# A graph layer on one core: 16 of the 128 columns of each copied group move to GpSimd

## The chip, the cores and the metric

The kernel runs on one core of a Trainium2 chip. The metric is the device time of one execution in microseconds (us). The engines are written as the profile writes them: PE (TensorE, the matmuls; PEld are its weight loads), DVE (VectorE), ACT (ScalarE), POOL (GpSimd) and SP (SyncE, which here only starts transfers). Each engine has a queue of its own, which takes the engine's instructions in their order; where it does something itself (loading addresses into registers, waiting for a second semaphore) the trace has rows for PEq, DVEq, ACTq and POOLq.

## The reference

One message-passing layer of a graph network with a residual and a layer norm, for 12,500 nodes of 64 features and 200,000 edges of 32 features. The edges come sorted by their target, `dst`.

```python
msg_in   = concatenate([x[src], x[dst], edge], axis=-1)      # 64 + 64 + 32 features
messages = relu(msg_in @ mW1 + mb1) @ mW2 + mb2              # 160 -> 128 -> 64
agg      = segment_sum(messages, dst, 12500)
upd      = relu(concatenate([x, agg], axis=-1) @ uW1 + ub1) @ uW2 + ub2
out      = layernorm(x + upd)                                # over the 64 features
```

## The kernel before

**Tables and tiles.** A first stage computes two tables in DRAM, `tab_a` = x times the source rows of mW1 and `tab_b` = x times its target rows with the bias, one row of 128 for each node. After that an edge needs only row `src` of `tab_a`, row `dst` of `tab_b` and its own 32 features times the edge rows of mW1. Edges are worked on in tiles of 128; six tiles are a group, and there are 261 groups. In the hidden layer a group is the PSUM tile `pc`, 128 edges by six blocks of 128.

**One group.** For each tile, `edge_part` issues one product over 64 rows (L413): 32 rows are edge features and the weights for them, 32 are a selection matrix and a window of `tab_b` (the edges are sorted, so one window of 32 nodes holds all targets of a tile). The rows of `tab_a` come by `fetch` (L241): an indirect transfer on POOL's queue for each tile, a *gather*, brings the 128 rows that `src` names into the tile `xg` in SBUF. `node_part` adds them to `pc` by a product with the identity matrix (L442), 384 wide for three blocks at a time. `positive` (L466, DVE) takes the relu into `h`; `collect` multiplies `h` by selection matrices and so sums the edges of each node in PSUM (L506), beside a product that counts them (L502). After some groups, `update` and the functions that follow it compute the second MLP and the layer norm for 416 nodes or so and store them.

**Copied groups.** In 121 of the 261 groups (`COPIED`) the last two of the six tiles aren't gathered. The kernel keeps x transposed in SBUF, twice: `xtop` holds the 64 features of each node on partitions 0 to 63 and zeros below, `xbot` the same on partitions 64 to 127 with zeros above. For each pair of edges, one of either tile, one column of `xtop` and one of `xbot` are added into one column of the tile `xc` (128 columns; three buffers). As the nodes are known only at run time, their addresses are loaded into registers from the table `col_a`, two for each column (`addresses`, L359). The tile `xc` is then multiplied by the source rows of mW1 (L416, two products of 64 rows for the two tiles, right behind L413 of the same tile). Such a group needs four gathers, not six, and its identity product is 256 wide.

**Who copies.** ACT copies the first `singles(j)` columns of copied group number j, 64 or (for one j in six) 72, by an activation with the second column as its bias (`singly`, L383). DVE copies the rest, by an or of the two columns (`joined`, L391). On both a load of 16 addresses stands in front of eight columns. POOL copies nothing.

**Pace.** The columns of a group are spread over several steps. `progress(s)` is the number of copied groups, with fractions, that are done after step s, by the rates in `PACE` (about half a group in each step); `portion(s, own)` gives the columns of an engine's share that fall on step s, rounded to eights (`CHUNK`). Copied group c is the one whose copying ends in step c - 3; the list is filled so:

```python
    while progress(s) >= len(COPIED) + 1 and s + 3 < FINAL:
        COPIED.append(s + 3)
```

**The main loop.** The order within each engine is the order in which the code is written (nothing is reordered). Step s of 258 issues, in turn: the gathers of group s + 8, the transfers of windows of `tab_b` for group s + 2, `node_part(s)`, `collect(s - 1)`, DVE's columns in three or four parts with the selection matrices and the relu of group s between them, `edge_part(s + 1)`, and ACT's columns. The gathers of a step are tied to products of that step: the first is free, the second waits for L442 of group s, the others for products of `collect(s - 1)` (and, where there are six, of `edge_part(s + 1)`). So POOL's gathers run about eight groups ahead of their use, in a pace set by TensorE. A tile `xg` may be refilled once its reader is done.

The functions that the change touches:

Of the kernel before, what the change touches and what calls it, by code (L numbers as in the profile page):

```python
# [10 lines left out]
F32 = mybir.dt.float32  # L11
I32 = mybir.dt.int32
AF = mybir.ActivationFunctionType
ALU = mybir.AluOpType
AX = mybir.AxisListType
ET = mybir.EngineType

P = 128
# [57 lines left out]
OFFS = 4  # L76
SBASE = (33556480, 33554432)
CBASE = 33566720
PACE = ((3, 0.474), (50, 0.501), (130, 0.479), (170, 0.465), (261, 0))
FINAL = 258  # L80
SUMMED = 255

# [1 line left out]
def progress(s):  # L84

    return sum(r * max(0, min(s + 1, b) - a) for (a, r), (b, _) in zip(PACE, PACE[1:]))

# [8 lines left out]

def singles(j):

    return 72 if j % 6 == 0 else 64

# [27 lines left out]
def gnn_kernel(ctx: ExitStack, tc: tile.TileContext, x1T, x, eT, e_rows, src, src_row, dst, dst_row, wlist, wrow, wnext, whalf,  # L130
# [24 lines left out]
    nc = tc.nc  # L155
# [57 lines left out]
    def frees(s):  # L213

        a = (XG + 1) // 2 + s - XG - ROWB
        return min(2 * a + 1, XG - 1) if a < (XG + 1) // 2 else XG + a - (XG + 1) // 2
# [4 lines left out]
    def gathered_tiles(s):  # L221
        return tiles(s)[:SUB - 2 * (s in COPIED)]

    def gather(s):

        if s >= XG or s % 2 == 0:
            buf = rows.tile([P, SUB, DH], F32, name="xg")
        else:
            buf = xg[s - 1][0]
        if s < XG:  # L230
            a = buf.rearrange("p k (b d) -> p (k b) d", d=D)[:, s % 2 * SUB:(s % 2 + 1) * SUB, :]
        else:
            a = buf.rearrange("p (b k) d -> p k b d", b=2)
        xg[s] = buf, a
        return [(s, i) for i in range(len(gathered_tiles(s)))]

    def fetch(unit, behind=None):

        s, i = unit
        t, a = s * SUB + i, xg[s][1]  # L240
        ins = nc.gpsimd.indirect_dma_start(  # L241
            out=a[:, i, :] if s < XG else a[:, i // 2, i % 2, :], out_offset=None, in_=A[:, :] if s >= XG else x[:, :],
            in_offset=bass.IndirectOffsetOnAxis(ap=src_s[:, t:t + 1], axis=0))
        if behind is not None:
            tc.add_manual_dep(ins.ins, behind.ins.name,
                              mybir.DependencyInfo(mybir.DependencyClass.Sync, mybir.DependencyReason.DATA), reason="pace")

    with tc.tile_pool(name="work", bufs=2) as work, tc.manual_schedule():
# [43 lines left out]
        def load(g):  # L292

            for b in range(2):
                q = EK[b]
                nc.sync.dma_start(L[g][q:q + DE], eT[g, b])
# [48 lines left out]
        def portion(s, own):  # L345

            found = []
            for j, c in enumerate(COPIED):
                total = own(j)
                lo, hi = (min(max(int((progress(s + d) - j) * total / CHUNK + 1e-6) * CHUNK, 0), total) for d in (-1, 0))  # L350
                if lo < hi:
                    if c not in xc:
                        xc[c] = work.tile([P, P], F32, name="xc", bufs=3)
                    found.append((xc[c], c - LEAD, lo, hi, j))
            return found

        def addresses(k, a, m, engine):

            _, v = nc.values_load_multi_w_load_instructions(  # L359
                col_a[k % P:k % P + 1, k // P].rearrange("k e b -> k (e b)")[:, 2 * a:2 * m], engines=[engine], min_val=XBASE,  # L360
                max_val=YBASE + LAST, skip_runtime_bounds_check_because="sources are node numbers")
            v = [w.with_bounds(min_val=base, max_val=base + LAST, guaranteed_mod_val=0, out_of_modulus=4)
                 for w, base in zip(v, (XBASE, YBASE) * (m - a))]
            return [(e, x8[:, bass.ds(v[2 * (e - a)] - XBASE, 4)], y8[:, bass.ds(v[2 * (e - a) + 1] - YBASE, 4)])
                    for e in range(a, m)]

        def share(todo, part, of):

            c = CHUNK // 2
            n = max(int(len(todo) / of / c + 0.5), 1) * c  # L370
            todo = todo[part * n:(part + 1) * n if part + 1 < of else None]
            while todo:
                o, k, a = todo[0]
                m = min(len([t for t in todo if t[1] == k]), CHUNK // 2)
                todo = todo[m:]
                yield o, k, a, a + 2 * m
# [7 lines left out]

        def joined(s, part, of):

            todo = [(o, k, singles(j) + e) for o, k, lo, hi, j in portion(s, lambda j: P - singles(j))
                    for e in range(lo, hi, 2)]
            for o, k, a, m in share(todo, part, of):
                for e, top, bot in addresses(k, a, m, ET.DVE):  # L390
                    nc.vector.tensor_tensor(o[:, e:e + 1].bitcast(I32), top.bitcast(I32), bot.bitcast(I32),  # L391
                                            op=ALU.bitwise_or)

        xc = {}

# [156 lines left out]
        def update(u):  # L552

            n = width(u)
            pu = shut.pop(u)[:, :n]
            if u not in pus:
                from_nodes(u, pu)
            nc.tensor.matmul(pus[u], w2u, sums_s[u % 2][:, :n], start=False, stop=True)  # L558
# [195 lines left out]
        for u in first[:AHEAD]:  # L754
            fetch(u)
# [140 lines left out]
        for s in range(FINAL):  # L896
            g, j = divmod(s, SUP // SUB)
            units = []
            while gathered < NSUB and frees(gathered) < s and gathered <= s + XG:
                units += gather(gathered)  # L900
                gathered += 1
            paced = s > 0 and s + 1 < NSUB and 0 < len(units) <= SUB
            for u in units[:1] if paced else units:
                fetch(u)
            units = units[1:] if paced else []
            def earlier(n):

                return next((u for d, u in due.items() if u + 2 < K and s - d == n and (n < 2 or u + 3 < K)), None)
            windows(s + 2)
            added = node_part(s)  # L910
            if units and added is not None:
                fetch(units.pop(0), added)
            if s:
                done = collect(s - 1)
                n = (len(units) + 1) // 2
                for k in range(n):
                    fetch(units.pop(0), done[(k + 1) * len(done) // n - 1])
            if s in due:
                update(due[s])
            for d, u in due.items():  # L920
                if d + 2 == s and u + 2 < K:
                    residual(u)
            ahead = j == 1 and g + 2 < NSUP
            parts_of = 4 if ahead else 3
            joined(s, 0, parts_of)
            if ahead:
                select_rows(g + 2)
                load(g + 2)
                joined(s, 1, parts_of)
            positive()  # L930
            joined(s, parts_of - 2, parts_of)
            for stage, n in ((statistics, 3), (deviation, 4)):
                if earlier(n) is not None:
                    stage(earlier(n))
            if ahead:
                select(g + 2)
                counts(g + 2)
            if s + 1 in due and due[s + 1] + 2 < K:
                close_counts(due[s + 1])
            if s == 0:  # L940
                loadd(2)
            if j == 1 and g + 3 < NSUP:
                loadd(g + 3)
            if chunks and s >= BS and chunks[0] < NCH + NB * (s + 1 - BS) / (SUP // SUB * (GE - 1) - BS):
                chunk_b(chunks.pop(0), [Bv])
            if s in due and due[s] + 1 < K:
                carry(due[s] + 1)
            if s + 1 < XG:
                transpose(s + 1)
            done = edge_part(s + 1)  # L950
            for k, u in enumerate(units):
                fetch(u, done[(k + 1) * len(done) // len(units) - 1])
            units = []
            if earlier(4) is not None:
                norm(earlier(4))
            if s + 2 in due and due[s + 2] + 1 < K:
                columns(due[s + 2])
            rest(s)
            joined(s, parts_of - 1, parts_of)
            if s + 1 in due and due[s + 1] + 2 < K:  # L960
                close_sums(due[s + 1])
            singly(s, 0, 1)
            if earlier(2) is not None:
                squares(earlier(2))
            if s in due and due[s] + 2 < K:
                activated(due[s])
            for u in units:
                fetch(u)
            if earlier(4) is not None:
                store(earlier(4))  # L970

# [44 lines left out]
    with tc.If(flag > 0), tc.tile_pool(name="gen", bufs=1) as up:  # L1016
# [90 lines left out]
        with tc.For_i(0, NB, 1) as c:  # L1107
# [24 lines left out]
            o = up.tile([P, D], F32, name="o")  # L1132
# [49 lines left out]
```

## Time and profile before

| | |
|---|---|
| three runs | 2130.83, 2136.61, 2140.01 us; median 2136.61 |
| the profiled execution | 2134.32 us, of which the span of the trace is 2132.5 us |
| granted clock of TensorE, mean | 0.786 |
| PE, PEld busy | 1665.4 us (78%), 1259.0 us (59%) |
| DVE busy | 1162.9 us (55%), 8400 instructions |
| ACT busy | 1583.4 us (74%), 8069 instructions |
| POOL busy | 1250.4 us (59%), 1330 instructions |
| gathers | 1273 from `tab_a`, 0.944 us each, and 48 from x, 1.000 us each |
| columns copied on ACT and on DVE | 7912, 0.280 us each, and 7576, 0.154 us each |

How the rows of the profile read: a group of instructions is named by its line, its engine, its operation and the tiles that it writes and reads, then how often it came, its busy time and the mean of one in ns, and behind the bar the idle time of the engine just ahead of them and what ended it; "issue" there means that nothing in the profile ended it. Rows of a queue (POOLq, DVEq) give the shortest, the median and the longest duration in ns. A row of a timeline is a start, a duration, and what ran; in square brackets stands the idle time before it. A row of a stretch gives busy time and count of an engine, then granted clock, the share of the transfer engines and GB/s.

### The profile page before, as it was taken

The numbers are of one execution on the slowest core, as the hardware profiler recorded it, in microseconds if no ns is written. First come the engines' busy times: TensorE is split into PE (matmuls) and PEld (weight loads), VectorE is DVE, ScalarE is ACT, GpSimd is POOL, SyncE is SP. The second block draws the span as 40 slices with busy tenths as digits, with TensorE's granted clock in tenths as the row PEclk, the third lists the DMA queues.
The fourth block names the chain that finished last, engine by engine and source line by source line (L and its number), as shares of the span: only waits on it lengthen the run. The fifth ranks groups of instructions, "written<-read, shape, count | busy, mean of one in ns | idle before, by whom it ended". The sixth has DMA issues, their size and how long they took to land.

```text
span 2132.5 us, 48222 instructions
## 1 busy us (share of the span) xinstructions
PE 1665.4 (78%) x10730; PEld 1259.0 (59%) x10730; DVE 1162.9 (55%) x8400; ACT 1583.4 (74%) x8069; POOL 1250.4 (59%) x1330
## 2 busy tenths in 40 slices
PE   3676887787787787878777878878776888888888
PEld 2564665565565556656656656656555666656666
DVE  2436555555555565565555545555554556555555
ACT  4396977759769688788786877777876868787774
POOL 6665665666665665655655555565556566666660
PEclk8677787787786777777877778787887878788779
DMA  8623333322223232232222323333332333333332
GB/s 227 185 73 85 87 95 90 106 75 80 74 75 81 73 83 75 74 86 78 77 82 81 85 77 89 83 91 84 81 90 75 87 85 94 87 93 88 90 88 54
DMA packets 207647, 190.04 MB, mean 89 GB/s; under 512 B 57813, under 2 KB 173997, under 8 KB 207357
## 3 DMA queue, kind: packets, MB, share of 16 engines
q0 software_dynamic: 42272, 85.08, 15.6%
q1 hardware_dynamic: 150396, 92.86, 15.5%
q10 hardware_dynamic: 14690, 8.99, 1.5%
q8 instruction: 90, 1.47, 0.3%
q14 instruction: 199, 1.63, 0.3%
HBM read 168.76 MB, written 18.02 MB: 88 GB/s over the span
## 4 chain that ended last, share of the span: by engine, by line
PE 50%; issue 16%; DVE 12%; another core or an unknown queue 3%; DVEq 2%; POOL 0%; ACT 0%; DMA 0%; ACTq 0%; POOLq 0%
PE sums L506 16%; PE pc L442 12%; PE pc L413 10%; DVE xc L391 6%; DVE h L466 3%; PE cnt L502 2%; PE cps L580 2%; PE cps L578 2%; DVE l L275 2%; PE sums L565 2%; DVEq L359 2%; PE sums L558 1%; PE pc L416 1%; PE cnt L500 1%
## 5 line engine op out<-in xcount | busy, mean ns | idle before, releaser
L241 POOL DMA_INDIRECT xg<-tab_a,src_s x1273 | 1201.4, 944 | 809.4 <-issue 266.0
L383 ACT ACTIVATE xc<-xtop,xbot 128x1 f32 x7912 | 1501.3, 280 | 172.7 <-issue 149.4
L391 DVE TENSOR_TENSOR xc<-xtop,xbot 128x1 int32 x7576 | 634.7, 154 | 504.9 <-issue 489.6
L506 PE MATMUL sums<-band,h 128*128 128x96 f32 x3126 | 529.7, 322 | 143.1 <-issue 91.3
L506 PEld LDWEIGHTS sums<-band,h 128*128 128x128 f32 x3126 | 466.4, 228 | 172.9 <-issue 106.3
L442 PE MATMUL pc<-xg,band 128*128 128x256 f32 (+1 forms) x988 | 445.8, 581 | 29.1 <-issue 27.5
L413 PE MATMUL pc<-rhs,l 64*128 64x128 f32 x3126 | 366.8, 351 | 79.3 <-issue 66.1
L413 PEld LDWEIGHTS pc<-rhs,l 64*128 64x128 f32 x3126 | 290.0, 235 | 127.0 <-issue 94.9
L466 DVE TENSOR_SCALAR h<-pc 128x768 f32<-128x768 f32 x247 | 235.0, 952 | 167.8 <-remote 62.4
L442 PEld LDWEIGHTS pc<-xg,band 128*128 128x128 f32 x988 | 215.5, 241 | 145.1 <-issue 100.2
L502 PEld LDWEIGHTS <-one 128*1 128x1 bf16 x1563 | 59.0, 81 | 247.2 <-issue 242.7
L275 DVE TENSOR_TENSOR l<-l,cps 128x768 f32<-128x768 int32 (+1 forms) x134 | 127.0, 947 | 136.2 <-remote 31.8
L502 PE MATMUL cnt<-band,one 128*1 128x32 bf16 x1563 | 95.4, 180 | 69.9 <-issue 68.8
L587 ACT ACTIVATE y<-cps 128x256 f32<-128x256 f32 (+1 forms) x36 | 13.6, 379 | 162.2 <-issue 106.8
L570 ACT ACTIVATE hTu<-sums,ub_s 128x416 f32<-128x416 f32 (+1 forms) x36 | 21.6, 600 | 136.0 <-remote 41.7
L416 PE MATMUL pc<-band,xc 64*128 64x128 f32 x484 | 78.3, 314 | 14.5 <-issue 13.3
L283 DVE TENSOR_TENSOR band<-cps,drc 128x384 f32<-128x384 f32 x131 | 71.4, 545 | 20.1 <-PE pc L413 15.8
L675 PE MATMUL pb<-band,xtop 64*128 64x128 f32 x200 | 44.1, 383 | 48.4 <-issue 20.9
L416 PEld LDWEIGHTS pc<-band,xc 64*128 64x128 f32 x484 | 65.2, 228 | 15.6 <-issue 15.5
L675 PEld LDWEIGHTS pb<-band,xtop 64*128 64x128 f32 x200 | 37.4, 276 | 52.5 <-issue 28.7
L241 POOL DMA_INDIRECT xg<-in_x,src_s x48 | 48.0, 1000 | 25.6 <-issue 14.4
L580 PE MATMUL cps<-u2c,hTu 128*128 128x64 f32 x284 | 51.3, 329 | 10.1 <-issue 9.8
(108 smaller groups left out, 636.4 us busy)
## 6 DMA issues: line engine op xcount, KB each, us to landing
l<-in_dst_row SPq DMA_DIRECT2D x262, 96.0 KB
l<-in_eT SPq DMA_DIRECT2D x262, 96.0 KB
xg<-tab_a,src_s POOLq DMA_INDIRECT x1273
rhs<-tab_b SPq DMA_DIRECT2D x361, 32.0 KB
tab_b<-tb SPq DMA_DIRECT2D x13, 512.0 KB
rhs<-tab_b SPq DMA_DIRECT2D x387, 16.0 KB
tab_a<-tb ACTq DMA_DIRECT2D x12, 512.0 KB
out<-y SPq DMA_DIRECT2D x35, 128.0 KB
```

Of the source, the lines that this page charges most:

```text
L241: ins = nc.gpsimd.indirect_dma_start(out=a[:, i, :] if s < XG else a[:, i // 2, i % 2, :], out_offset=None, in_=A[:, :] if s >= XG else x[ ...
L275: nc.vector.tensor_tensor(l[r], l[r].bitcast(I32), node[r].unsqueeze(2).broadcast_to([r.stop - r.start, SUP // 2, P]), op=ALU.is_equal)
L383: nc.scalar.activation(o[:, e:e + 1], top.bitcast(F32), AF.Identity, bias=bot.bitcast(F32))
L391: nc.vector.tensor_tensor(o[:, e:e + 1].bitcast(I32), top.bitcast(I32), bot.bitcast(I32), op=ALU.bitwise_or)
L413: done = nc.tensor.matmul(pc[:, b, k, :], L[g][q:q + 64, m, :], rhs[g % 2][q:q + 64, w, :], start=k == 0, stop=ends and not copied)
L416: done = nc.tensor.matmul(pc[:, b, k, :], xc[s][q:q + 64], w1a[q:q + 64], start=False, stop=ends)
L442: added = nc.tensor.matmul(pc[:, b, :m], ident, a[:, b, :m], start=False, stop=True)
L466: nc.vector.tensor_scalar(h, pc, 0.0, None, op0=ALU.max)
L502: nc.tensor.matmul(pn8[:, bass.ds(cs[i] - CBASE, 4 * WIN)].bitcast(F32), one, SB[g][:, k0 + i, :, 1], start=False, stop=ends and i == n - 1)
L506: made.append(nc.tensor.matmul(ps8[:, bass.ds(ws[i] - SBASE[u % 2], 4 * WIDE * WIN)].bitcast(F32), h[:, i % 2, i // 2, :], widened(g, k0 + i),
L580: nc.tensor.matmul(py[:, i], hT[:, i * P:(i + 1) * P], u2c, start=False, stop=i + 1 == blocks(u))
L675: nc.tensor.matmul(pb[:, h, i, :], (xbot if h else xtop)[64 * h:64 * h + 64, (c + HB * h + i) * P:(c + HB * h + i + 1) * P], w[64 * h:64 * ...
```

## The change

`BYPOOL` = 16 columns of each copied group, the last 16, go to POOL, by a new function `aside`. For each two of them it puts one piece of work into the list `also`: a load of four addresses into POOL's registers (`addresses`) and two additions of one column of `xtop` and one of `xbot`, as float. `fetch` takes one such piece off the list ahead of each gather that it issues; what is left at the end of a step is issued there. At the start of step s, `aside(s - 1)` fills the list. ACT's share goes to 64 or 56 columns, DVE's is what is left, and the rates in `PACE` are higher, so that 134 groups are copied and not 121.

By the list of instructions this makes of 7912 columns on ACT 7776, of 7576 on DVE 7232 (of 947 loads 904), of none on POOL 2144 with 1072 loads, and of 1321 gathers 1295. The full diff:

```diff
@@ -76,7 +76,8 @@
-PACE = ((3, 0.474), (50, 0.501), (130, 0.479), (170, 0.465), (261, 0))
+PACE = ((3, 0.49), (20, 0.54), (50, 0.56), (130, 0.536), (170, 0.52), (261, 0))
+BYPOOL = 16
 FINAL = 258
@@ -96,7 +97,7 @@
 def singles(j):
 
-    return 72 if j % 6 == 0 else 64
+    return 64 if j % 4 == 0 else 56
@@ -234,10 +235,14 @@
+    also = []
+
     def fetch(unit, behind=None):
 
         s, i = unit
         t, a = s * SUB + i, xg[s][1]
+        if also:
+            also.pop(0)()
         ins = nc.gpsimd.indirect_dma_start(
...
@@ -384,12 +389,22 @@
         def joined(s, part, of):
 
-            todo = [(o, k, singles(j) + e) for o, k, lo, hi, j in portion(s, lambda j: P - singles(j))
+            todo = [(o, k, singles(j) + e) for o, k, lo, hi, j in portion(s, lambda j: P - BYPOOL - singles(j))
                     for e in range(lo, hi, 2)]
...
+        def aside(s):
+
+            def two(o, k, e):
+                for f, top, bot in addresses(k, e, e + 2, ET.Pool):
+                    nc.gpsimd.tensor_tensor(o[:, f:f + 1], top.bitcast(F32), bot.bitcast(F32), op=ALU.add)
+
+            for o, k, lo, hi, _ in portion(s, lambda j: BYPOOL):
+                for e in range(P - BYPOOL + lo, P - BYPOOL + hi, 2):
+                    also.append(lambda o=o, k=k, e=e: two(o, k, e))
@@ -896,6 +911,8 @@
         for s in range(FINAL):
             g, j = divmod(s, SUP // SUB)
             units = []
+            if s:
+                aside(s - 1)
...
@@ -966,6 +983,8 @@
             for u in units:
                 fetch(u)
+            while also:
+                also.pop(0)()
             if earlier(4) is not None:
```

In the rows below, the words in brackets are the semaphores that an instruction waits for: `DMASW` a gather, `DMAHW` another transfer, `PE`, `DVE`, `Activation` and `Pool` an engine's instructions. On POOL before, in the middle of the run, there are gathers alone, most of them tied to a product of TensorE:

```order
L241 DMA xg<-tab_a,src_s 128x128 [waits DMASW4_49]
L241 DMA xg<-tab_a,src_s 128x128 [waits DMASW5_49,PE_49]
L241 DMA xg<-tab_a,src_s 128x128 [waits DMASW6_49,PE_49]
L241 DMA xg<-tab_a,src_s 128x128 [waits DMASW7_49,PE_49]
L241 DMA xg<-tab_a,src_s 128x128 [waits DMASW0_49]
L241 DMA xg<-tab_a,src_s 128x128 [waits DMASW1_49,PE_49]
```

On POOL in the changed kernel, at the same place (`xc` is the copied tile; L246 is the gather, L364 the load of four addresses, L403 the addition):

```order
L364 TENSOR_LOAD col_a
L403 TENSOR_TENSOR xc<-xtop,xbot 128x1 [waits DVE_49,Activation_49,Pool_49]
L403 TENSOR_TENSOR xc<-xtop,xbot 128x1
L246 DMA xg<-tab_a,src_s 128x128 [waits DMASW2_49]
L364 TENSOR_LOAD col_a
L403 TENSOR_TENSOR xc<-xtop,xbot 128x1 x2
L246 DMA xg<-tab_a,src_s 128x128 [waits DMASW3_49,PE_49]
L364 TENSOR_LOAD col_a
```

Each gather now has a load and two additions in front of it, and the first addition into a new `xc` tile also waits for DVE and ACT.

On PE before, the products of a copied group's fifth and sixth tile with the copied columns (`rhs` is the window of `tab_b`, `l` the selection and edge features, `band` in L416 the source weights), and the identity products that follow them:

```order
L413 MATMUL pc<-rhs_79,l_80 128x128 [waits DMAHW7_49]
L413 MATMUL pc<-rhs_79,l_80 128x128
L416 MATMUL pc<-band,xc 128x128 [waits Activation_49]
L413 MATMUL pc<-rhs_79,l_80 128x128
L416 MATMUL pc<-band,xc 128x128
L442 MATMUL pc<-xg,band 128x256 [waits DMASW6_49,DMASW4_49]
L442 MATMUL pc<-xg,band 128x256 [waits DMASW7_49,DMASW5_49]
```

The same in the changed kernel (L428, L431 and L457 are the former L413, L416 and L442):

```order
L428 MATMUL pc<-rhs_79,l_80 128x128 [waits DMAHW7_49]
L428 MATMUL pc<-rhs_79,l_80 128x128
L431 MATMUL pc<-band,xc 128x128 [waits Activation_49,Pool_49]
L428 MATMUL pc<-rhs_79,l_80 128x128
L431 MATMUL pc<-band,xc 128x128
L457 MATMUL pc<-xg,band 128x256 [waits DMASW2_49,DMASW0_49]
L457 MATMUL pc<-xg,band 128x256 [waits DMASW3_49,DMASW1_49]
```

The order of the products is as it was; the first product with the copied columns waits for POOL too.

## The prediction

> **What bounds the kernel now.** I read the page's busy times first, then the chain of work that ended last, then the groups by line, and after that the places of the change: POOL's timeline, the address loads and the chain inside one stretch.
>
> ```profile
> span 2132.5 us, 48222 instructions
> PE 1665.4 (78%) x10730; PEld 1259.0 (59%) x10730; DVE 1162.9 (55%) x8400; ACT 1583.4 (74%) x8069; POOL 1250.4 (59%) x1330
> PEclk8677787787786777777877778787887878788779
> PE 50%; issue 16%; DVE 12%; another core or an unknown queue 3%; DVEq 2%; POOL 0%; ACT 0%; DMA 0%; ACTq 0%; POOLq 0%
> PE sums L506 16%; PE pc L442 12%; PE pc L413 10%; DVE xc L391 6%; DVE h L466 3%; PE cnt L502 2%; PE cps L580 2%; PE cps L578 2%; DVE l L275 2%; PE sums L565 2%; DVEq L359 2%; PE sums L558 1%; PE pc L416 1%; PE cnt L500 1%
> L241 POOL DMA_INDIRECT xg<-tab_a,src_s x1273 | 1201.4, 944 | 809.4 <-issue 266.0
> L383 ACT ACTIVATE xc<-xtop,xbot 128x1 f32 x7912 | 1501.3, 280 | 172.7 <-issue 149.4
> L391 DVE TENSOR_TENSOR xc<-xtop,xbot 128x1 int32 x7576 | 634.7, 154 | 504.9 <-issue 489.6
> ```
>
> No engine is full. The chain is half TensorE's, at a granted clock of some 0.8, and most of the rest is DVE's; ACT and POOL are on it with 0%. The 258 steps of the main loop take about 8 us each, and the chain passes from TensorE to DVE and back. Where it is on DVE, the stretch looks like this (first the chain of the stretch by line, then DVE's own rows in it, then what the address loads take):
>
> ```profile
> by line: DVE xc L391 32.1%; issue 32.0%; DVE h L466 12.4%; DVEq L359 6.7%; DVE l L275 6.5%; DVE band L283 3.7%; PE pc L416 3.5%; PE pc L413 2.3%; DVE y L610 1.5%; DVE ss L596 1.2%; DVE rs L608 0.7%
> ...
> 1057.71 0.65 DVE L391 TENSOR_TENSOR xc<-xtop,xbot 128x1 int32 x8
> 1059.20 0.64 DVE L391 TENSOR_TENSOR xc<-xtop,xbot 128x1 int32 x8 [0.84 <-issue]
> ...
> L359 ACTq TENSOR_LOAD <-col_a x989: 1011/1042/2582, 103.6 to 2094.8; - x198
> L359 DVEq TENSOR_LOAD <-col_a x947: 1093/1124/2120, 81.7 to 2094.3; - x190
> ```
>
> A batch of eight copied columns on DVE is one load of 16 addresses, 1.124 us, and eight operations that end within 0.65 us. The load of the next batch begins before the eight are done, so from batch to batch it is 1059.20 - 1057.71 = 1.49 us, of which 0.84 shows as idle "issue". On the chain there is as much issue time as L391 time (32.0% against 32.1%). Carried over to the whole run, copying on DVE holds 6% (L391) + 6% (its issue time) + 2% (DVEq L359) = 14% of the chain, 14% of 2132.5 = 298 us, or 298 / 1.49 = 200 of the 947 batches.
>
> **The change part by part.** *DVE's columns.* They go from 7576 to 7232, 947 batches to 904: 43 fewer, 4.5%. If none were on the chain the gain is 0; if all were, it is 43 x 1.49 = 64 us. I take the share that is on it, 4.5% of 298 = 14 us off.
>
> *ACT's columns.* 7912 to 7776, 136 fewer at 0.28 us each at most, 38 us of ACT. ACT holds 0% of the chain, so the gain is 0; what hides it is DVE and TensorE, and nothing is late if that cover goes.
>
> *The 13 further copied groups.* Each loses two gathers, 26 in all; and its identity product has two blocks a half instead of three, for two more 64-row products.
>
> ```profile
> L442 PE MATMUL pc<-xg,band 128*128 128x384 f32 x512 | 276.8, 672 | 16.5 <-issue 16.5
> L442 PE MATMUL pc<-xg,band 128*128 128x256 f32 x476 | 169.0, 482 | 12.6 <-issue 11.0 <-DMA xg<-tab_a,src_s 1.4
> L416 PE MATMUL pc<-band,xc 64*128 64x128 f32 x484 | 78.3, 314 | 14.5 <-issue 13.3 <-ACT xc L383 0.6 <-DMA xg<-tab_a,src_s 0.5
> L413 PEldq EVENT_SEMAPHORE  x342: 51/51/831, 72.0 to 2117.7; - x171
> ```
>
> There are 512 / 4 = 128 whole groups and 476 / 4 = 119 copied ones: 276.8 / 128 = 2.16 us against 169.0 / 119 + 78.3 / 121 = 2.07 us. So 13 x 0.09 = 1 us off TensorE, which is on the chain.
>
> *One more wait on the copied product.* L416 (L431 in the change) now waits for POOL too, and a second semaphore is a wait of its own in TensorE's queue, 51 ns as at L413. For 134 groups that is 7 us if each is on the chain and 0 where the products before it still run. With half the chain TensorE's and products mostly queued, I take 2 us.
>
> *POOL.* This is the part that decides. POOL now only gathers:
>
> ```profile
> 1008.25 0.94 POOL L241 DMA_INDIRECT xg<-tab_a,src_s  x1 [0.30 <-issue]
> 1009.49 0.95 POOL L241 DMA_INDIRECT xg<-tab_a,src_s  x1 [0.30 <-issue]
> 1010.74 0.94 POOL L241 DMA_INDIRECT xg<-tab_a,src_s  x1 [0.30 <-issue]
> ...
> L241 POOL DMA_INDIRECT xg<-in_x,src_s x48 | 48.0, 1000 | 25.6 <-issue 14.4 <-ACT tb L685 9.8 <-DMA src_s<-in_src 1.2
> ...
> 1000.00:1200.00 200.00, 117.90 (x126) 0.78 0.30 83
> ```
>
> A gather costs 1.25 us from start to start. 1321 of them are 1651 us; the idle time before them is 809.4 + 25.6 = 835 us, of which 1321 x 0.30 = 396 belongs to the gathers themselves, so 439 us are waits. 26 gathers fewer add 26 x 1.25 = 32. The waits, mostly for TensorE's products that pace the gathers, are thus 471 us of room. (In the 200 us from 1000 it is 200 - 117.9 - 126 x 0.30 = 44 us.)
>
> Added are 1072 loads of four addresses and 2144 additions of a 128x1 column. POOL's loads and additions do not stand in the trace; the nearest rows are these:
>
> ```profile
> L1014 POOLq TENSOR_LOAD <-flag_i x1: 502/502/502, 2084.9 to 2084.9; - x1
> L1014 PEldq TENSOR_LOAD <-flag_i x1: 312/312/312, 2126.2 to 2126.2; - x1
> L478 PEldq TENSOR_LOAD <-lists x522: 501/508/1135, 78.4 to 2122.2; - x174
> ...
> masks.py:199 POOL TENSOR_SCALAR_AFFINE_SELECT band<-band 128x128 f32<-128x128 f32 x1 | 0.3, 291 | 0.1
> L751 POOL IOTA pidx_i<- 128x1 int32 x1 | 0.1, 139 | 0.0
> L1174 POOL MEMSET const-float32-0.0<- 128x1 f32 x1 | 0.1, 98 | 0.3 <-issue 0.3
> ```
>
> The load: one address takes POOL 0.50 us, and on TensorE's queue four take 0.20 us more than one, so 0.70 us; its ends are 0.50 and ACT's 1.04 for sixteen. It is work of the queue, not of the engine, and on DVE the next load begins while the operations before it still run. Beside a gather of 1.25 us it is hidden on the engine, and I cost it at nothing. If that cover is missing it is 1072 x 0.70 = 750 us.
>
> The addition: between 0.098 us (a MEMSET of the same 128x1, which reads nothing) and 0.291 us (the select over 128x128, the one row in which POOL reads a tensor). DVE's operation on the same columns takes 0.154, POOL's IOTA into 128x1 0.139. I take 0.15, by these two rows: 2144 x 0.15 = 322 us of 471 us of room, POOL's work then being 1295 x 1.25 + 322 = 1941 us, 91% of the span. The room is used up at 471 / 2144 = 0.22 us for one addition; as pairs stand only in front of the first four gathers of a step, not all of the room can be filled, and I put the point at 0.20. Above it each 0.01 us costs 21 us: at 0.25 us it is +107, at 0.291 +195. Below it the cost is 0, if the columns are in time, which the next row tests.
>
> The last two of POOL's columns of copied group c stand in front of the fourth gather of step c - 2, and L416 of group c runs in step c - 1. A place where this is close:
>
> ```profile
> 997.82 0.94 POOL L241 DMA_INDIRECT xg<-tab_a,src_s  x1 [1.52 <-PE pc L442]
> 999.07 0.94 POOL L241 DMA_INDIRECT xg<-tab_a,src_s  x1 [0.30 <-issue]
> ...
> 999.81 0.49 PE L416 MATMUL pc<-band,xc 64*128 64x128 f32 x4
> ```
>
> The fourth gather starts at 999.07, 0.74 us ahead of the product. Two additions there move the gather by 0.3 us and end before it, so they are in time. The gather ahead of it waited for a product (1.52 us), and a wait takes up what was added before it. Being late at 134 groups by at most two additions would cost 134 x 0.3 = 40 us; I take 0, since the waits on POOL are frequent and the place shown is a narrow one.
>
> *The sum*: -14 (DVE) + 0 (ACT) - 1 (products) + 2 (waits) + 0 (loads and additions) = -13 us. The profiled execution took 2134.32 us, 2.3 less than the median of the three runs, so the forecast on that median is 2136.6 - 13 = 2123.6, given as 2123: 0.6% faster. A measurement of this kernel can tell about 0.5%, 10.7 us, from no change. The forecast's own range is 2085 to 2126: all 43 batches on the chain, less a little, at one end, and the bound of "faster" at the other.
>
> **The rivals.** *POOL becomes the bound (slower).* An addition of more than 0.20 us fills POOL's waits. For it: POOL goes from 77% of the span (1651 us) to 91% already at 0.15 us, the one row in which it reads a tensor is 0.291, and POOL's columns must be there a step later, while its gathers run eight groups ahead. Against it: the rows of 128x1 lie at 0.10 to 0.14 us. At 0.25 us the time is 2136.6 - 13 + 107 = 2231, at 0.22 us 2166, at 0.291 us 2319; I put it at 2150 to 2320. It shows as gathers back to back with TensorE waiting for POOL at L431.
>
> *The columns of DVE and POOL collide (slower).* In this kernel DVE's L391, L275 and L283 read two tensors, and so does each of POOL's additions. If one had to sit out the other, an addition would meet L275 (127.0 us of 0.947 us each) for 127.0 / 2132 x 0.47 = 0.03 us on average, L283 (71.4 us of 0.548 each) for 0.01 and a run of eight L391 (634.7 us, 0.65 each) for 634.7 / 2132 x 0.33 = 0.10.
>
> ```profile
> L275 DVE TENSOR_TENSOR l<-l,cps 128x768 f32<-128x768 int32 x128 | 121.3, 947 | 133.7 <-remote 31.8 <-PE pc L442 26.8 <-PE pc L416 23.2
> L283 DVE TENSOR_TENSOR band<-cps,drc 128x384 f32<-128x384 f32 x130 | 71.2, 548 | 20.1 <-PE pc L413 15.8 <-remote 2.8 <-issue 1.4
> ```
>
> Then an addition is 0.15 + 0.14 = 0.29 us and the time 2136.6 - 13 + 193 = 2317. Nothing in the trace shows POOL and DVE waiting for each other. [...]
>
> *The load is not hidden (slower).* If POOL's queue takes no load while a gather runs, 750 + 322 - 471 = 601 us are left over: 2725. Against it: on DVE and ACT loads run beside their operations.
>
> *The relief comes to nothing (no change).* DVE's 43 batches lie where TensorE is the later one, or the wait at L431 eats what they give: 2126 to 2147. For it: the chain is half TensorE's, at a clock that this change doesn't touch.
>
> **How the numbers follow.** Forecast 0.42; POOL the bound 0.27; collision 0.05; load not hidden 0.05; no change 0.21. Faster is thus 0.42, same 0.21, slower 0.27 + 0.05 + 0.05 = 0.37. The likeliest is the forecast, 2123. The range goes from 2085, below which I leave 0.03, to 2240, above which lie the two last slow cases (0.09) and the part of POOL the bound beyond an addition of 0.25 us (0.08).
>
> **What the profile of the change would show.** If right: L403 near 0.15 us, gathers with waits left (some 150 us, from 439), POOL loads of 0.6 to 0.7 us that start while a gather runs, 904 loads on DVE still 1.49 us apart, less DVE in the chain, and L431 waiting for POOL hardly at all. If POOL is the bound: its waits near 0, POOL in the chain, and TensorE or DVE idle behind L431. Wrong would also be a DVE row L396 much over 0.154 us, which would be the collision seen from DVE's side.

## The result, and the profile after

The change took 2116.43 us (median of four runs, 2115.05 to 2121.47) beside 2136.15 us before: a ratio of 0.9914, interval 0.9887 to 0.9941. That is 20 us less, where the prediction gave 13 (2123 us). In later runs the kernel before took 2134 us on one chip, but 1687 to 1688 us on three others. On one of these three the same change was run again, and was 14.5% slower than before. So the result has two halves, and each needs its own reading.

From the page of the change, in the run of the result (the span and the busy times, the chain by engine and by line, then groups):

```profile
span 2115.0 us, 51339 instructions
PE 1715.3 (81%) x10782; PEld 1302.3 (62%) x10782; DVE 1170.4 (55%) x8055; ACT 1558.6 (74%) x7933; POOL 1606.6 (76%) x3448
PE 60%; issue 18%; DVE 15%; another core or an unknown queue 3%; ACT 2%; DVEq 1%; DMA 1%; POOL 0%; ACTq 0%; SPq 0%; POOLq 0%
PE sums L521 18%; PE pc L457 15%; PE pc L428 13%; DVE xc L396 7%; DVE h L481 3%; PE cnt L517 3%; PE cps L595 2%; PE pc L431 2%; PE cps L593 2%; DVE l L280 2%; PE sums L580 2%; PE sums L573 1%; DVEq L364 1%; DVE band L288 1%
...
L246 POOL DMA_INDIRECT xg<-tab_a,src_s x1247 | 1196.7, 960 | 421.5 <-issue 132.0
L396 DVE TENSOR_TENSOR xc<-xtop,xbot 128x1 int32 x7232 | 644.4, 157 | 451.5 <-issue 437.9
...
L403 POOL TENSOR_TENSOR xc<-xtop,xbot 128x1 f32 x2144 | 360.6, 197 | 19.6
```

POOL is busy for 356 us more and still holds 0% of the chain: here its work was hidden, as forecast. DVE's copies (L396) hold 7% of the chain where the page of before shows 6%, but the two shares can't be compared as they stand. The chain of before breaks off: it goes back from the end as far as 368 us and covers 1760 of the 2132 us, so its shares add up to 83%. Of the part that is covered, the copies hold 7.6% before and 7.2% after, and TensorE 60% in both (not half, as the prediction read it). Whether 14 us came off there can't be read from this; a run below tells. An addition takes 0.197 us, just under the 0.20 us at which POOL was to become the bound. What it costs is less. From POOL's timeline and the row of its loads:

```profile
1010.25 0.33 POOL L403 TENSOR_TENSOR xc<-xtop,xbot 128x1 f32 x2
1010.73 0.97 POOL L246 DMA_INDIRECT xg<-tab_a,src_s  x1 [0.15 <-issue]
1011.72 0.33 POOL L403 TENSOR_TENSOR xc<-xtop,xbot 128x1 f32 x2
1012.20 0.96 POOL L246 DMA_INDIRECT xg<-tab_a,src_s  x1 [0.15 <-issue]
1013.47 0.95 POOL L246 DMA_INDIRECT xg<-tab_a,src_s  x1 [0.31 <-issue]
...
L364 POOLq TENSOR_LOAD <-col_a x1072: 314/329/1207, 116.4 to 2073.8; - x179
```

With a pair in front of it a gather starts 1012.20 - 1010.73 = 1.47 us after the one before; without, about 1.25. The two additions overlap (0.33 us together), and some of that lies in the 0.30 us that stand between two gathers anyway: a pair costs 0.22 us, an addition 0.11. The load of four addresses takes 0.33 us and runs mostly beside a gather: 1001 of the 1072 loads overlap one. Over the whole trace 985 gathers have one pair in front of them. What POOL waits beyond such distances (above the shortest tenth of the distances of each kind) went from 439 to 221 us.

### The profile page after: what moved, and what is told of

Its sections match the earlier page's. It is cut to its first block, busy times and chain, and to the rows that moved or that the text cites. A ratio compares the mean times of both kernels' runs of the same rounds, so it can differ in the third digit from the quotient of the medians.

```text
span 2115.0 us, 51339 instructions
## 1 busy us (share of the span) xinstructions
PE 1715.3 (81%) x10782; PEld 1302.3 (62%) x10782; DVE 1170.4 (55%) x8055; ACT 1558.6 (74%) x7933; POOL 1606.6 (76%) x3448
## 4 chain that ended last, share of the span: by engine, by line
PE 60%; issue 18%; DVE 15%; another core or an unknown queue 3%; ACT 2%; DVEq 1%; DMA 1%; POOL 0%; ACTq 0%; SPq 0%; POOLq 0%
PE sums L521 18%; PE pc L457 15%; PE pc L428 13%; DVE xc L396 7%; DVE h L481 3%; PE cnt L517 3%; PE cps L595 2%; PE pc L431 2%; PE cps L593 2%; DVE l L280 2%; PE sums L580 2%; PE sums L573 1%; DVEq L364 1%; DVE band L288 1%
## 5 line engine op out<-in xcount | busy, mean ns | idle before, releaser
L388 ACT ACTIVATE xc<-xtop,xbot 128x1 f32 x7776 | 1475.6, 280 | 171.7 <-issue 96.0
L246 POOL DMA_INDIRECT xg<-tab_a,src_s x1247 | 1196.7, 960 | 421.5 <-issue 132.0
L396 DVE TENSOR_TENSOR xc<-xtop,xbot 128x1 int32 x7232 | 644.4, 157 | 451.5 <-issue 437.9
L521 PE MATMUL sums<-band,h 128*128 128x96 f32 x3126 | 535.6, 325 | 106.7 <-issue 75.0
L521 PEld LDWEIGHTS sums<-band,h 128*128 128x128 f32 x3126 | 474.6, 232 | 133.3 <-issue 87.3
L457 PE MATMUL pc<-xg,band 128*128 128x256 f32 (+1 forms) x988 | 445.5, 580 | 17.9 <-issue 16.7
L428 PE MATMUL pc<-rhs,l 64*128 64x128 f32 x3126 | 387.4, 355 | 80.9 <-issue 67.1
L428 PEld LDWEIGHTS pc<-rhs,l 64*128 64x128 f32 x3126 | 301.8, 237 | 135.6 <-issue 103.0
L403 POOL TENSOR_TENSOR xc<-xtop,xbot 128x1 f32 x2144 | 360.6, 197 | 19.6
L457 PEld LDWEIGHTS pc<-xg,band 128*128 128x128 f32 x988 | 219.7, 245 | 129.1 <-issue 77.9
L280 DVE TENSOR_TENSOR l<-l,cps 128x768 f32<-128x768 int32 (+1 forms) x134 | 126.7, 946 | 134.3 <-PE pc L457 35.7
L431 PE MATMUL pc<-band,xc 64*128 64x128 f32 x536 | 100.9, 336 | 24.9 <-issue 22.5
L431 PEld LDWEIGHTS pc<-band,xc 64*128 64x128 f32 x536 | 80.9, 242 | 32.2 <-issue 29.4
L288 DVE TENSOR_TENSOR band<-cps,drc 128x384 f32<-128x384 f32 x131 | 71.1, 543 | 21.1 <-remote 20.6
L246 POOL DMA_INDIRECT xg<-in_x,src_s x48 | 48.2, 1003 | 26.2 <-issue 13.1
```

The costliest lines, as they stand in the source:

```text
L246: ins = nc.gpsimd.indirect_dma_start(out=a[:, i, :] if s < XG else a[:, i // 2, i % 2, :], out_offset=None, in_=A[:, :] if s >= XG else x[ ...
L280: nc.vector.tensor_tensor(l[r], l[r].bitcast(I32), node[r].unsqueeze(2).broadcast_to([r.stop - r.start, SUP // 2, P]), op=ALU.is_equal)
L288: nc.vector.tensor_tensor(s[:, :nt], slot.unsqueeze(1).broadcast_to([P, nt, WIN]), drc[:, g * SUP:g * SUP + nt].unsqueeze(2).broadcast_to( ...
L388: nc.scalar.activation(o[:, e:e + 1], top.bitcast(F32), AF.Identity, bias=bot.bitcast(F32))
L403: nc.gpsimd.tensor_tensor(o[:, f:f + 1], top.bitcast(F32), bot.bitcast(F32), op=ALU.add)
L428: done = nc.tensor.matmul(pc[:, b, k, :], L[g][q:q + 64, m, :], rhs[g % 2][q:q + 64, w, :], start=k == 0, stop=ends and not copied)
```

## The experiments

**Which part gives the gain.** The change does two things: POOL takes columns, and 13 more groups are copied. Four runs on one chip (before: 2134.44 us there) do them apart. All start from the changed kernel. Three of them go back to the rates of before, so that 121 groups are copied:

```diff
 # 121 groups, POOL copies 16 columns of each
-PACE = ((3, 0.49), (20, 0.54), (50, 0.56), (130, 0.536), (170, 0.52), (261, 0))
+PACE = ((3, 0.474), (50, 0.501), (130, 0.479), (170, 0.465), (261, 0))
```

> POOL copies 16 columns as in the change, but the pace is that of before: 121 copied groups. DVE then copies 6528 columns (7576 before), ACT 7024 (7912). Theory A (as predicted: the gain is DVE's columns on the chain, 298 us for 7576 of them): 1048 / 7576 x 298 = 41 us off before, some 2095 us, faster than the change. Theory B (the gain comes from the 13 further copied groups, which take gathers and the wider products away; relief of the copying engines as such is worth nothing): like before, 2136 us.

Measured: 2138.21 us, ratio 1.0018 (1.0008 to 1.0028). POOL's copying alone gives nothing; if anything it costs 0.2%.

```diff
 # 134 groups, POOL copies nothing
-BYPOOL = 16
+BYPOOL = 0
-    return 64 if j % 4 == 0 else 56
+    return 72 if j % 6 == 0 else 64
```

> 134 copied groups at the pace of the change, but POOL copies nothing; ACT copies 8760 columns, DVE 8392. Theory A: DVE has 816 columns more than before, 816 / 7576 x 298 = 32 us, less 1 us of products: some 2167 us. Theory B: like the change, 2116 us.

Measured: 2121.23 us, ratio 0.9938 (0.9920 to 0.9956). The 13 groups alone give 13 us. The change itself lies 5 us lower, and the two intervals overlap.

```diff
 # 121 groups by the same PACE, POOL's columns taken from ACT alone
-    return 64 if j % 4 == 0 else 56
+    return 56 if j % 6 == 0 else 48
```

> 121 groups; POOL's 16 columns are all taken from ACT (5976 columns, 7912 before), DVE copies its 7576 as before. Theory A (only DVE's columns are on the chain): 2136 us, no change. Theory C (ACT's columns set the time, though the chain of waits gives ACT 0%): 1936 x 0.28 = 542 us of ACT less; if a tenth of it is in the way, 54 us off, some 2082 us.

Measured: 2135.95 us, ratio 1.0011 (1.0000 to 1.0022).

```diff
 # 121 groups by the same PACE, POOL's columns taken from DVE alone
-    return 64 if j % 4 == 0 else 56
+    return 72 if j % 6 == 0 else 64
```

> 121 groups; POOL's 16 columns are all taken from DVE (5640 columns, 7576 before), ACT copies its 7912 as before. Theory A: 1936 / 7576 x 298 = 76 us off, some 2060 us. Theory C: no change, 2136 us.

Measured: 2139.89 us, ratio 1.0027 (1.0016 to 1.0038). A quarter of DVE's columns off its hands, 1936, and the time is no shorter. Theory A, the prediction's reason, expected 2060 us and falls. Theory C falls with the run before it. Theory B holds: the gain is that of the 13 groups. The trace of this run shows where DVE's relief went, though not why: TensorE waits 39 us less for DVE than in the kernel before (67 us, 106 before), but is itself busy for 47 us more (1712.0 us, 1665.4 before) with the same number of products.

**What in a copied group saves time, and how far the room goes.** Four more kernels, on another chip. The first two start from the kernel before and leave part of the sum out, the rows gathered for two tiles of 42 groups:

```diff
+LESS = [s for s in range(9, 250) if s not in COPIED][::3]
 # node_part: the identity product
-                    m = SUB // 2 - (s in COPIED)
+                    m = SUB // 2 - (s in COPIED or s in LESS)
 # and for the second run, gathered_tiles too
-        return tiles(s)[:SUB - 2 * (s in COPIED)]
+        return tiles(s)[:SUB - 2 * (s in COPIED or s in LESS)]
```

> The kernel before (121 copied groups), but in 42 of the 140 whole groups the identity product is 256 wide, not 384, so the gathered rows of the last two tiles are left out of the sum; all gathers stay. Theory B1 (a copied group saves time by TensorE's work): 42 x (2.16 - 1.42) = 31 us of products less; if all of it counts 2105 us, if half of it 2120. Theory B2 (a copied group saves time by its two missing gathers): 2136 us.

> As the run with the narrower identity products in 42 whole groups, and the last two tiles of these groups are not gathered either: 84 gathers fewer, no columns copied for them. Theory B1: like the run with the narrower products alone. Theory B2: 26 gathers fewer went with 13 us (134 groups without POOL's columns against before), 0.5 us each, so 84 x 0.5 = 42 us off, some 2094 us.

Measured: 1684.84 and 1685.41 us beside 1687.32 us for the kernel before: 0.9984 (0.9971 to 0.9998) and 0.9986 (0.9971 to 1.0001). The 1687 us for the kernel before is another level than the 2134 to 2136 so far. Here the question could not be answered: the narrower products, alone or with 84 gathers fewer, change the time by less than 0.2%, 0.3% at the ends of the intervals. So it stays open where the 13 us come from at the other level. But the trace of the first of the two runs, the one with all gathers, shows what the kernel is at this level; no trace of the kernel before itself was taken here. From its page:

```profile
span 1684.8 us, 48222 instructions
PE 1377.5 (82%) x10730; PEld 1090.1 (65%) x10730; DVE 1146.9 (68%) x8400; ACT 1552.7 (92%) x8069; POOL 1252.8 (74%) x1330
...
L242 POOL DMA_INDIRECT xg<-tab_a,src_s x1273 | 1203.7, 946 | 392.6 <-issue 256.6
L392 DVE TENSOR_TENSOR xc<-xtop,xbot 128x1 int32 x7576 | 631.4, 153 | 444.2 <-issue 424.8
...
L503 PE MATMUL cnt<-band,one 128*1 128x32 bf16 x1563 | 79.9, 178 | 1.9 <-issue 1.9
```

The idle time ahead of a gather is 392.6 + 21.8 (48 gathers from x) = 414 us, of which 1321 x 0.30 = 396 belongs to the gathers: POOL's waits are 20 us, not 439. ACT is busy for 92% of the span, not 74%. DVE is as full: 1146.9 us of work and 424.8 us of "issue" ahead of its copies, which is the time of its address loads, are 93% of the span. TensorE waits 1.9 us for "issue" ahead of the counting products, where it had waited 68.8. The timeline of the kernel before, at 2134 us, shows what these waits are:

```profile
322.02 0.18 PE L502 MATMUL cnt<-band,one 128*1 128x32 bf16 x1 [0.23 <-issue]
322.74 0.18 PE L502 MATMUL cnt<-band,one 128*1 128x32 bf16 x1 [0.54 <-issue]
323.45 0.18 PE L502 MATMUL cnt<-band,one 128*1 128x32 bf16 x1 [0.54 <-issue]
324.17 0.24 PE L502 MATMUL cnt<-band,one 128*1 128x32 bf16 x3 [0.54 <-issue]
```

These products wait for no semaphore; the last three of this run are all there within 0.24 us, but the ones before start 0.71 us apart. Take the distances of over 0.6 us between neighbouring products of one line, where neither the second product nor its weight load waits for a semaphore: there are 377 in the trace of before, 344 us in all, against 57 and 42 us here (most of these are wide products at half clock; one 384 wide takes 0.85 us at half clock in the trace of before, 0.49 at full, by the median). The difference, 302 us, is the larger part of the 447 us between 2134 and 1687; the rest was not taken apart. A distance of 0.67 to 0.76 or of 1.38 to 1.46 us came 177 times there, 211 times in the change, and 22 times here. These distances, in which TensorE stands idle without a cause in the trace, are called its gaps below.

The third kernel takes the change further, the fourth doubles POOL's additions:

```diff
 # 159 groups, 24 columns on POOL, 56 on ACT, 48 on DVE
+PACE = ((3, 0.49), (20, 0.645), (50, 0.668), (130, 0.64), (170, 0.62), (261, 0))
+BYPOOL = 24
+    return 56
 # the change, each addition twice
                 for f, top, bot in addresses(k, e, e + 2, ET.Pool):
-                    nc.gpsimd.tensor_tensor(o[:, f:f + 1], ...)
+                    for _ in range(2):
+                        nc.gpsimd.tensor_tensor(o[:, f:f + 1], ...)
```

> A version that goes further: 159 copied groups, POOL copies 24 columns of each, ACT 56, DVE 48, so that ACT copies 8904, DVE 7632 and POOL 3816 columns. If each further copied group saves the 1.0 us that 13 groups saved (13 us), whatever the cause, 38 x 1.0 = 38 us off before: some 2096 us, 20 below the change. If the copying engines are full by then, POOL above all (1243 gathers x 1.25 + 3816 x 0.11 = 1974 us of work), it is no faster than the change, 2116 or more.

> The change with each of POOL's additions made twice, into the same column: 4288 in place of 2144, the loads as they are. In the change a pair lengthens the distance of two gathers by 0.22 us (1.47 against 1.25), of 0.33 us that it takes, the rest of it lies in the 0.30 us between gathers; POOL's waits beyond that are 221 us. Two more additions in a pair are 0.33 us more, 1072 x 0.33 = 354 us. If POOL's waits are room to be filled, the first 221 us are free and 133 are left over: some 2250 us. If POOL's work is hidden as long as the engine is not full (its work would be 1900 + 354 = 2250 us), the same; if waits elsewhere shrink with it, 2116.

Measured: 2089.54 us, ratio 1.2385 (1.2360 to 1.2411), and 2812.55 us, ratio 1.6670 (1.6626 to 1.6715), both to before at 1687. The first number sits near the 2096 expected, but that was worked out for a kernel before at 2136, so it means the opposite: POOL hardly rests (30 us of waits beyond the distances that its work sets). From the groups of the version with 159 copied groups:

```profile
L403 POOL TENSOR_TENSOR xc<-xtop,xbot 128x1 f32 x3816 | 607.9, 193 | 24.0 <-issue 1.0
...
L431 PE MATMUL pc<-band,xc 64*128 64x128 f32 x636 | 146.0, 371 | 400.8 <-POOL xc L403 400.6
```

TensorE waits 401 us for POOL's columns. In the run with doubled additions it is 993 us, and two more of them cost more than the 0.33 us that was put down: a gather with four additions in front starts 2.32 us after the one before on average, 0.84 later than with two (1.48 in the change on such a chip). Here is POOL's timeline:

```profile
1500.64 0.87 POOL L404 TENSOR_TENSOR xc<-xtop,xbot 128x1 f32 x4
1502.02 0.96 POOL L246 DMA_INDIRECT xg<-tab_a,src_s  x1 [0.51 <-issue]
```

Four additions, two of them into the column just written, take 0.87 us and not 2 x 0.33, and 0.51 us of idle time follows. This run repeats columns, so it doesn't price four columns; the pieces of ten additions in the run with 159 groups do, at 1.36 us for ten (2.61 from gather to gather).

**The change where TensorE does not starve** (where it has none of these gaps). The change and the version with 159 groups, again:

> The change, unaltered, beside the kernel before on the same chip. In the last call the kernel before took 1687 us and not 2136: TensorE's products followed each other without the gaps of 0.7 and 1.4 us that stand in its trace of 2134 us, and POOL's gathers came nearly back to back (waits of 21 us where a kernel with all gathers was profiled there). Theory D (POOL has room only where TensorE starves): with before at 1687 us the change is bound by POOL, 985 gathers with a pair at 1.47, 291 without at 1.25 and the rest 50, some 1860 us plus 48 gathers' start, so 1870 to 1950 us, over 10% slower; with before at 2136 us the ratio is 0.99 again. Theory E (the change's effect is the same few parts in a thousand everywhere): 0.99 in either case.

> The version with 159 copied groups and 24 columns on POOL, again. Its own POOL work is 933 distances of 1.47, 80 of 2.02, 142 of 2.6 and 89 of 1.25 us, 2015 us; where the kernel before took 1687 us it took 2089. Theory D: 2089 us again wherever TensorE does not starve; where before takes 2136 us, 2100 to 2140, as POOL's 2015 us then fill the time nearly. Theory E with each copied group worth 1.0 us: 2098 where before takes 2136.

Measured on another chip, before at 1687.88 us: the change 1929.72 us, ratio 1.1449 (1.1422 to 1.1476); the other 2090.46 us, 1.2392 (1.2369 to 1.2415). Theory D holds, theory E falls. From the page of the change here, the busy times, the chain by engine, and three groups:

```profile
span 1927.0 us, 51339 instructions
PE 1553.5 (81%) x10782; PEld 1207.7 (63%) x10782; DVE 1161.6 (60%) x8055; ACT 1536.2 (80%) x7933; POOL 1608.7 (83%) x3448
PE 41%; POOL 21%; issue 19%; DVE 10%; POOLq 4%; ACT 3%; DMA 1%; DVEq 1%; ACTq 0%; SPq 0%
...
L246 POOL DMA_INDIRECT xg<-tab_a,src_s x1247 | 1197.5, 960 | 234.0 <-issue 135.2
L403 POOL TENSOR_TENSOR xc<-xtop,xbot 128x1 f32 x2144 | 362.1, 198 | 18.3
L431 PE MATMUL pc<-band,xc 64*128 64x128 f32 x536 | 117.9, 358 | 279.8 <-POOL xc L403 279.6
```

POOL's rows are those of the result, 0.960 and 0.198 us, but POOL is on the chain with 21% and TensorE waits 280 us at L431, where it waited 2 us. From gather to gather it is 985 x 1.48 + 291 x 1.30 + 43 us for 18 longer pieces = 1879 us, and the span is 1927. In the run at 1685 us the gathers lie 1664 us from the first to the last, so 215 of the 242 us that the change adds lie between POOL's gathers.

**The two parts apart, where TensorE does not starve.** The runs with 134 groups without POOL and with 121 groups and POOL, again, on a third such chip (before: 1687.98 us):

> 134 copied groups, POOL copies nothing (8760 columns on ACT, 8392 on DVE), again. Where before takes 2136 us: 0.994 of it, as measured. Where before takes 1687 us: theory D1 (there the gathers, back to back, are the bound): 26 gathers fewer, 26 x 1.25 = 32 us off, 1655 us; theory D2 (there ACT and DVE, ACT at 92% of the span, are as near to their limit): 106 loads with 8 columns more on ACT, 106 x 1.40 = 148 us, or 102 more on DVE, 102 x 1.49 = 152 us, some 1830 us.

> 121 groups as before, POOL copies 16 columns of each, again. Where before takes 2136 us: 1.002 of it, as measured. Where before takes 1687 us, POOL's work is 955 distances of 1.47 and 365 of 1.25 us, 1860 us, and some 50 us lie outside of it (as in the change, 1879 of 1930): theory D expects 1910 us, the change's 1930 less nothing but its longer pieces. If it is the 13 further groups that cost the change its time there, 1687 us.

Measured: 1835.74 us, ratio 1.0886 (1.0856 to 1.0916), and 1925.69 us, ratio 1.1401 (1.1374 to 1.1428). Theory D2 was right, D1 wrong: 13 more groups on ACT and DVE alone cost 148 us. From the run with 134 groups, the rows of ACT and of DVE for the 200 us from 1000 (busy time, count, granted clock, share of the transfer engines, GB/s), and, for the whole run, what DVE's copies and TensorE waited for longest:

```profile
1000.00:1200.00 200.00, 197.56 (x1053) 0.86 0.36 99
1000.00:1200.00 200.00, 137.31 (x1086) 0.86 0.36 99
...
DVE xc L396 <- issue: 507.5, 729, 2.1
...
PE sums L521 <- DVE h L481: 170.2, 94, 4.0
```

ACT is busy for 197.56 of 200 us. DVE is busy for 137.31, and its address loads ("issue" ahead of L396) take 59 of the rest, so it has next to no room either. In the whole run TensorE is idle for 381 us and waits for DVE in 360 of them, mostly for the relu, which stands behind the copies in DVE's queue. Whether ACT or DVE sets the time was not taken apart; both columns grew. POOL has 173 us of waits in the whole run (above 1.25 us from gather to gather): its gathers are not what binds. In the run with 121 groups and POOL it is POOL again, with TensorE waiting for it:

```profile
PE pc L431 <- POOL xc L403: 309.3, 98, 7.9
```

Put together, each as a ratio to before on the same chip:

| | before at 2134 to 2136 us | before at 1687 to 1688 us |
|---|---|---|
| 134 groups, POOL copies 16 (the change) | 0.991 | 1.145 |
| 134 groups, POOL copies nothing | 0.994 | 1.089 |
| 121 groups, POOL copies 16 | 1.002 | 1.140 |
| 159 groups, POOL copies 24 | not run | 1.239 |

Of the three versions run at both levels, none is better at both.

## Why the prediction was right, and where its reasons were not

The forecast of 13 us less came near the measured 20 us by luck: the largest term of its sum gave nothing, and a term of 1 us gave 13.

*DVE's columns: 14 us off.* This step failed. The chain of waits put 14% of its time on DVE's copies, and the prediction took a proportional share of it (counted piece by piece, copies, loads and their "issue" hold 275 of the 1760 us that the chain covers, so the 298 us were read about rightly). The run that takes 1936 columns from DVE was to gain 76 us by that reckoning and lost 0.3%. A share of the chain says where the time was while it was spent, not what goes when that work goes: TensorE waited 39 us less for DVE in that run, and was busy for 47 us more.

*The 13 groups: 1 us off.* Mis-sized: 13 us, measured by themselves. The prediction priced only TensorE's busy time of a copied group against a whole one. What else a copied group saves there was not found. At the other level the same 13 groups cost 148 us.

*ACT's columns: 0.* Right at that level: the time with 1936 columns fewer lies within 0.2% of before. At the other, ACT is nearly full at 121 groups (92%), and so is DVE with its loads (93%); the rows of the prediction, 74% and 55% busy, did not show it.

*One more wait on the copied product: 2 us.* The second wait stands in TensorE's queue 115 times, 51 ns each, 6 us in all; what of that delays TensorE is not known. For POOL's columns themselves TensorE waits 2.1 us at L431.

*POOL: loads and additions 0.* Right there. Of its numbers, the gathers kept 221 us of waits, not some 150; the load was put at 0.70 us and took 0.33; the addition was put at 0.15 us, took 0.197, and lengthens POOL's work by 0.11. By the prediction's reckoning, in which the whole of an addition is added to POOL's work, 0.197 us would have left 471 - 2144 x 0.197 = 49 us; so the bound of 0.20 us, which 0.197 just keeps, was set too low. The 471 us were read correctly from the trace, and this step carried most. But they are no room of the kernel as such. Where TensorE has no gaps the waits are 20 us, against 985 x 0.22 + 21 for the longer pieces - 32 for 26 fewer gathers = 206 us of added work; the time there rose by 242. The rival "POOL becomes the bound" named gathers back to back and TensorE waiting at L431; this is what the other chips show, by the room and not by the price of an addition.

*The collision of DVE and POOL* did not come. In the change, 970 additions ran beside a column copy of DVE, at 0.200 us on average, and 720 beside no instruction of DVE, at 0.196. DVE's copies took 154 ns beside an addition, 159 beside a gather and 152 while POOL was idle; that their mean went from 154 to 157 ns is thus not the additions' doing. POOL stands idle for 19.6 us in all ahead of the 2144 additions, so they were not held up before their start either. Beside the other two lines of DVE that the prediction names, L275 and L283 (L280 and L288 in the change), 168 and 122 additions took 0.197 and 0.194 us. The 0.14 us of the rival's sum rest on its assumption that one instruction sits out the other; no run shows that, and the trace shows no more than 2 to 3 ns (199.6 against 196.3 ns for an addition, 154.0 against 151.5 for a copy).

*The load not hidden* did not come either: a load of 0.33 us stands in front of each pair, and the 1.47 us from gather to gather have no room for it but beside the gather (0.96 + 0.33 for the pair leave 0.18).

What could have been seen ahead stands among TensorE's waits in the kernel before (what waited, for what, us in total, times, the longest):

```profile
PE sums L506 <- issue: 91.3, 136, 1.8
PE cnt L502 <- issue: 68.8, 106, 1.7
PE pc L413 <- issue: 66.1, 103, 2.3
```

Products that have nothing to wait for, and wait: of the 461 us that TensorE is idle in the kernel before, 318 us are "issue". The prediction gave 6% of the chain's 16% "issue" to DVE's loads and read nothing into the rest. Piece by piece, 214 of the 334 us are TensorE's and 107 us stand ahead of DVE's copies.

## What to carry to other kernels

Idle time of an engine is room only if one knows what keeps it idle: POOL's 439 us of waits were 20 us where TensorE had no gaps, and there the same additions made the kernel 14% slower. Count an engine's address loads as its work: DVE looked 68% busy and with its loads was as full as ACT (93% and 92%). Before work is spread over a further engine, take it off one engine alone and look whether the time moves at all; at the 2134 us level it did not, and no run showed that POOL's copying pays. A share of the chain of waits is no estimate of a gain: the share said 76 us, and the run lost 5.

## What the runs showed of the hardware

**The same program at 2134 and at 1687 us.** The traces at the first level have gaps between TensorE's instructions, often 0.71 or 1.42 us from start to start; the traces from three other chips have hardly any (no line of TensorE waits for "issue" for more than 9 us in all there, against 91 us in the kernel before). All executions of a kernel on one chip were at one level, and no chip on record was measured a second time, so whether the level goes with the chip or with the hour is open. Gathers, additions, loads and DVE's copies took the same at both: gathers 0.944 us in the kernel before and 0.946 in the run at 1685 us, the copies 0.154 and 0.153; in the change at 2116 and at 1930 us gathers 0.960 and 0.960, additions 0.197 and 0.198, POOL's loads 0.329 and 0.330 (median), DVE's 1.124 and 1.124. What makes the gaps was not found: they could not be switched on or off. The transfers on the queues that the page calls `instruction` are no explanation that the traces show: on the queue with most of them they take 0.42 us (median; 0.40 in the run at 1685 us), and 33 of 289 start in such a gap, where 41 would if they fell anywhere.

**In these traces TensorE's clock follows its own work.** Full and half clock come there in pieces of 3.41 us or a multiple (231 of 232 pieces in the kernel before, 217 of 218 in the change at 2116 us; the odd one is the last of the trace). Cut into pieces of 3.41 us, the change where TensorE has no gaps has 60 at full clock in which products were under way for less than half of the time: the next piece was at half clock in all 60. Of 213 with over 0.8, the next one was at full clock in all 213. From half clock it never went up after less than 0.8 (52 pieces), and in 77 of 158 after more than 0.9. In the kernel before, with gaps, it was 65 of 65, 175 of 175, 1 of 76 and 112 of 165. So waits cost twice in these runs: the mean granted clock is 0.889 in the run at 1685 us, 0.804 in the change at 1930, and 0.770 with 159 groups, though TensorE has less to do per microsecond there (6.4 products in the first, 5.6 in the second). The amount of waiting alone doesn't tell the clock: with 134 groups and nothing on POOL, TensorE is idle for 381 us at a clock of 0.854, and in the change for 368 us at 0.804. What kept the full clock often didn't suffice to get it back: after half-clock pieces with 0.8 to 0.9 it went up in 2 of 10 in that change and in 2 of 25 in the kernel before.
